# Two-bank score tiles and a new step plan in an attention and mixture-of-experts kernel

## The chip, the cores and the metric

The kernel runs on one core of a Trainium2 chip. The metric is the device time of one execution in microseconds (us). PE is TensorE (its weight loads are shown as PEld), DVE is VectorE, ACT is ScalarE, POOL is GpSimd, SP is the engine that issues most DMAs. PSUM, where PE writes, has 8 banks of 512 float32 in each of 128 partitions.

## What is computed

32 sequences of 256 tokens, model width 128. Each is layer-normed, then goes through one decoder block and a mixture of experts:

```python
x = layer_norm(hidden, ln1)                       # hidden: the layer norm of the input
hidden = attn(split_heads(q, k, v of x), causal) @ attn_proj_w + attn_proj_b + hidden
x = layer_norm(hidden, lnx)
hidden = attn(q of x, k and v of the encoder, logits added, tril + 2) @ x_proj_w + x_proj_b + hidden
hidden = hidden + gelu(layer_norm(hidden, ln2) @ fc_w + fc_b) @ mlp_proj_w + mlp_proj_b
x = x_input + layer_norm(hidden)
out = x + layer_norm(shared expert + top 2 of 8 experts, each (silu(a) * b) @ w2, of layer_norm(x))
```

Attention has 16 heads of width 8. The encoder's 256 keys and values are the same for all sequences. The softmax subtracts each query's own maximum.

## The kernel before, in words

The program has three stages: attention (lines 200 to 676), the MLP with the gate (line 786 on), the experts (line 909 on). Only the first one is changed.

Heads are laid out in four row groups of 32 partitions (g) with four heads each (j). A score product takes 32 partitions of one group and 128 columns of the array, so four products, one of each group, can run side by side. Each float32 query or key is kept as three bfloat16 parts, and the spare rows of a head hold the causal mask. Scores are computed twice. `maxima` (line 420) writes them by query into `sc` tiles, adds the mask on the diagonal with `strips`, and VectorE takes each query's negated maximum (line 443). `split` (446) makes three bfloat16 parts of the maxima on POOL, and `turned_maxima` (457) transposes them on PE. `weights` (477) computes the scores by key into `st` tiles, adds the maxima with `pick`, and ScalarE takes the exponential into `wt` (503). `weighted` (513) sums the values, 128 partitions by 32 columns of the array, into one `av` tile; a column of ones gives the softmax's sum. `back` (536) transposes and divides (547, 548), `turned_back` (551) transposes again, `joined` (559) multiplies by the output weights and adds to `h_all`.

Before all that a sequence is loaded (350), normed (`normed_in`, 361: statistics on VectorE, the power -0.5 on POOL in `rsqrt`, line 186), transposed (`turned`, 382), and projected (`projections`, 387). `projected` (240) splits queries and keys into parts on POOL (250 to 253), stores them in DRAM and loads them again in the layout of the heads, all by DMAs of the SP queue. `values` (404) makes the value tile `vpad`. For a self sequence `normed_in` makes two normed copies with two powers: `xn`, and the row `h_all` (lines 372 to 376); `biased` (378) adds the output bias to `h_all` on POOL.

A sequence's query work is cut into halves (412), one step each: 6 for a self, 8 for a cross sequence; its key work likewise (465). A half has two groups, so two `sc` tiles or two `st` tiles of one bank each. All PSUM tiles of all stages come from one pool of 8 banks, `ps` (159).

The order on PE is written out by hand: the loop at 662 takes two steps together, issues the products of up to two query halves and two key halves interleaved by group (`issue`, 569), then the reductions and exponentials (`after`), then the extra pieces of the two steps, with `weighted` last. VectorE, ScalarE and POOL are ordered by the framework, which also decides which free bank or buffer a tile gets, and each engine works strictly in its order. The steps come from the planner at 587 to 661: `on` puts a piece at a step, `full` at an even step, moved by one pair if a pair's cost passes 1.9. A sequence's key halves start LAG = 13 steps after its query halves; at most AHEAD = 7 sequences are begun and not yet at their cross attention; query and key buffers are used again after 4 sequences. In the regular part of the plan 14 steps (7 pairs) hold one self and one cross sequence.

## Time and profile before

| what | us |
|---|---|
| median of three runs | 1599.27 (1598.25 to 1602.11) |
| the profiled execution | 1591.84 |
| its span, first to last instruction | 1590.1 |
| PE busy | 1407.4 (89%) |
| PEld busy | 1099.7 (69%) |
| DVE busy | 1054.3 (66%) |
| ACT busy | 870.9 (55%) |
| POOL busy | 653.1 (41%) |
| DVE maxima, line 443, 896 instructions | 496.2 |
| ACT exponentials, line 503, 896 instructions | 420.7 |

The profiled execution is one run with the hardware profiler on. "Busy" is the time in which an engine executed something; matmuls are pipelined, so a busy PE is not PE at its peak. A row of the timeline has the start in us from the start of the span, the time in us, engine, source line, operation, output<-input, shape, the count of equal instructions that were merged, and in brackets the idle time before with what ended it. A row of the waits says which engine waited for what: us in total, times, longest. "issue" is time in which an engine waited for nothing that the profile shows.

### The profile page before, as it was taken

What the parts mean: (1) busy time and instruction counts of PE and PEld (TensorE: products, weight loads), DVE (VectorE), ACT (ScalarE), POOL (GpSimd) and SP (SyncE); (2) the same over time, 40 slices, a digit from 0 to 9 for tenths busy, and PEclk for the clock granted to TensorE, in tenths of its full rate; (3) what the DMA queues carried; (4) which work ended last, traced back from release to release, by engine and by line L of the source; (5) the groups of instructions that cost most, each with busy time, mean ns of one, the idle gap of its engine ahead of it and who ended that gap; (6) DMA issues with size and microseconds to landing.
All of it is one profiled execution on the core that took longest, in us unless ns stands there. A gap on an engine that the chain in (4) does not pass through costs nothing.

```text
span 1590.1 us, 74601 instructions
## 1 busy us (share of the span) xinstructions
PE 1407.4 (89%) x32988; PEld 1099.7 (69%) x32988; DVE 1054.3 (66%) x2955; ACT 870.9 (55%) x2032; POOL 653.1 (41%) x1475
## 2 busy tenths in 40 slices
PE   3678898898988988888999899799979999999997
PEld 2566677776777777777777787478756666666664
DVE  5647667776677776677776666267866666666665
ACT  1353566665666666666666655677734443433433
POOL 7435445444445444444444322378631212222112
PEclk8788999999999999999999989899979999999998
DMA  5632223232232232232222200500000000000000
GB/s 140 189 99 79 65 91 101 65 115 77 71 115 73 91 100 66 84 103 64 93 89 82 66 16 28 148 20 1 1 1 8 7 14 14 8 14 14 7 14 14
DMA packets 106037, 97.27 MB, mean 61 GB/s; under 512 B 4764, under 2 KB 105360, under 8 KB 105712
## 3 DMA queue, kind: packets, MB, share of 16 engines
q1 hardware_dynamic: 104432, 91.49, 18.7%
q8 instruction: 258, 4.23, 1.1%
q10 hardware_dynamic: 1280, 1.01, 0.2%
q14 instruction: 67, 0.55, 0.1%
HBM read 54.47 MB, written 37.77 MB: 58 GB/s over the span
## 4 chain that ended last, share of the span: by engine, by line
PE 66%; DVE 18%; POOL 6%; ACT 4%; issue 3%; DMA 3%; SPq 0%; POOLq 0%; ACTq 0%; DVEq 0%
DVE m L443 11%; PE av L525 11%; PE sc L580 9%; PE po L940 8%; PE pa L929 8%; PE pb L930 8%; PE st L580 7%; PE po L844 4%; PE pf L837 3%; PE pq L245 2%; POOL r L191 2%; ACT wt L503 2%; DVE st L182 2%; PE pa L541 1%; DVE xn L195 1%
## 5 line engine op out<-in xcount | busy, mean ns | idle before, releaser
L443 DVE TENSOR_REDUCE m<-sc 128x2 f32<-128x512 f32 (+2 forms) x896 | 496.2, 607 | 236.8 <-PE sc L580 207.3
L503 ACT ACTIVATE wt<-st 128x512 f32<-128x512 f32 (+1 forms) x896 | 420.7, 539 | 261.1 <-PE st L580 199.8
L580 PEld LDWEIGHTS <-qs 32*128 32x128 bf16 x6144 | 226.4, 95 | 96.7 <-issue 83.5
L580 PE MATMUL st<-mT,pick 32*128 32x256 bf16 (+2 forms) x2048 | 242.7, 245 | 3.8 <-issue 3.7
L580 PEld LDWEIGHTS <-strips 32*128 32x128 bf16 x7424 | 190.2, 94 | 21.8 <-issue 18.4
L940 PEld LDWEIGHTS po<-w,h 128*128 128x128 f32 x1152 | 154.7, 191 | 67.9 <-issue 49.5
L580 PE MATMUL sc<-kr,qs 32*128 32x256 bf16 (+1 forms) x3072 | 165.6, 250 | 33.4 <-DMA kr<-k 24.7
L580 PE MATMUL st<-qs,kr 32*128 32x128 bf16 (+1 forms) x3072 | 179.3, 248 | 8.3 <-issue 4.8
L580 PE MATMUL st<-qs,krx 32*128 32x130 bf16 (+1 forms) x3072 | 177.6, 243 | 7.4 <-issue 5.6
L580 PE MATMUL sc<-krx,qs 32*128 32x256 bf16 (+1 forms) x3072 | 178.9, 246 | 5.6 <-issue 2.6
L934 DVE SCALAR_TENSOR_TENSOR h<-pb,cols,sa 128x512 f32<-128x512 f32 x144 | 107.9, 749 | 113.7 <-ACT sa L932 88.8
L932 ACT ACTIVATE sa<-pa,cols 128x512 f32<-128x512 f32 x144 | 99.7, 693 | 147.3 <-PE pa L929 120.4
L940 PE MATMUL po<-w,h 128*128 128x128 f32 x1152 | 161.9, 277 | 0.0
L929 PE MATMUL pa<-h_all,w 128*128 128x512 f32 x288 | 150.7, 605 | 0.0
L930 PE MATMUL pb<-h_all,w 128*128 128x512 f32 x288 | 147.9, 595 | 0.0
L580 PE MATMUL sc<-strips 32*128 32x64 bf16 (+2 forms) x3840 | 140.2, 193 | 6.5 <-issue 6.4
L580 PE MATMUL st<-strips 32*128 32x64 bf16 (+2 forms) x3584 | 137.2, 193 | 8.7 <-issue 8.6
L954 POOL TENSOR_TENSOR z<-z 128x512 f32<-128x512 f32 x32 | 40.7, 1271 | 245.9 <-ACT z L950 245.9
L525 PE MATMUL av<-wt,vpadx 128*32 128x128 f32 (+1 forms) x4096 | 111.5, 252 | 32.2 <-DVE m L443 28.6
L191 POOL TENSOR_TENSOR r<-r,nhalf 128x2 f32<-128x2 f32 (+1 forms) x160 | 133.0, 837 | 9.9
L580 PEld LDWEIGHTS <-kr 32*128 32x128 bf16 x3072 | 118.1, 95 | 16.7 <-issue 13.9
L525 PEld LDWEIGHTS av<-wt,vpadx 128*32 128x32 f32 x4096 | 97.8, 112 | 44.4 <-DVE m L443 36.6
(162 smaller groups left out, 2649.8 us busy)
## 6 DMA issues: line engine op xcount, KB each, us to landing
kr<-k SPq DMA_DIRECT2D x32, 768.0 KB
k<-qkp SPq DMA_DIRECT2D x32, 576.0 KB
qs<-q SPq DMA_DIRECT2D x64, 256.0 KB
q<-qkp SPq DMA_DIRECT2D x64, 192.0 KB
x<-in_x_dram SPq DMA_DIRECT2D x32, 128.0 KB
x_all<-in_x_dram SPq DMA_DIRECT2D x8, 512.0 KB
out_dram<-y SPq DMA_DIRECT2D x16, 256.0 KB
w<-in_rw_dram SPq DMA_DIRECT2D x1, 1024.0 KB
```

What stands on the lines that cost most here:

```text
L191: nc.gpsimd.tensor_tensor(r, r, nhalf[:, 0:n], ALU.pow)
L443: nc.vector.tensor_reduce(m[:, g, js[0] : js[0] + n], t3, AX.X, ALU.max, negate=True)
L503: nc.scalar.activation(w[:, 0 : n * nq], t, AF.Exp)
L525: nc.tensor.matmul(av[32 * g : 32 * g + 32, j // 2, to : to + n], lhsT=self.vp[:, kb, g, WINDOW[j] : WINDOW[j] + 32], rhs=self.wts[kb, g, ...
L580: nc.tensor.matmul(dst, lhsT=lhsT, rhs=rhs, start=start, stop=False, skip_group_check=True)
L837: nc.tensor.matmul(pf, lhsT=wfc[:, f * P : (f + 1) * P], rhs=self.xT, start=True, stop=True)
L844: nc.tensor.matmul(po[:, i, :], lhsT=self.g[:, f, i * P : (i + 1) * P], rhs=wmlp[:, f, :], start=f == 0, stop=f == FF // P - 1)
L929: nc.tensor.matmul(pa, lhsT=w1[:, e, 0:D], rhs=rhs, start=True, stop=True)
L930: nc.tensor.matmul(pb, lhsT=w1[:, e, D : 2 * D], rhs=rhs, start=True, stop=True)
L932: nc.scalar.activation(sa, pa, AF.Silu, bias=col(C_B1 + 2 * e))
L934: nc.vector.scalar_tensor_tensor(h, pb, col(C_B1 + 2 * e + 1), sa, ALU.add, ALU.mult)
L940: nc.tensor.matmul(po[:, i, :], lhsT=h[:, i * P : (i + 1) * P], rhs=w2[:, e, :], start=True, stop=e < NE)
```

## The change

Six things are changed, all in attention:

- An `sc` tile is one tile of two banks for both groups of a half, and one VectorE reduction covers both.
- PSUM is cut for this stage into two such `sc` tiles (4 banks) and a pool of 4 banks for everything else. The pool of 8 is opened for the later stages.
- For a self sequence VectorE prepares both powers side by side, POOL takes one power of 128x4 (exponents 0.5 and -0.5), and `h_all` is made from `xn` with the output bias in one VectorE instruction. `biased` is left for cross sequences alone.
- The planner: LAG 15, AHEAD 8, pieces start earlier (loads at 28 steps ahead for 22, norms at 24 for 18), `weighted` has pairs of its own, which `full` avoids, and the plan is made four times so that it knows them. `turned_maxima` stands at least a pair later. Query and key buffers are free at the end of the key halves, and projections wait for that.
- `wt` tiles have two sizes: 18 of 512 columns and 8 of 260, for 22 of 512.
- Some preparations are moved: the two bias products to the head of PE's order, the clearing of the maxima frames behind the first four sequences' norms.

```diff
+    phalf = const.tile([P, 2, 2], F32, name="halves")
+    nc.gpsimd.memset(phalf[:, 0, :], 0.5)
+    nc.gpsimd.memset(phalf[:, 1, :], -0.5)
...
-    ps = ctx.enter_context(tc.tile_pool(name="ps", bufs=8, space=PSUM))
...
+        rings["sc"] = actx.enter_context(tc.tile_pool(name="ps_sc", bufs=2, space=PSUM))
+        rings["ps"] = actx.enter_context(tc.tile_pool(name="ps_a", bufs=4, space=PSUM))
...
-                    r1 = rsqrt(wk, mv, 1.0, EPS, "a")
-                    r2 = rsqrt(wk, mv, 1.0 + EPS, EPS * EPS, "b")
+                    r = wk.tile([P, 2, 2], F32, tag="rab", name="r")
+                    ratio, r2 = r[:, 0, :], r[:, 1, :]
+                    nc.vector.tensor_scalar(r2, mv[:, :, 1], 1.0 + EPS, EPS * EPS, ALU.mult, ALU.add)
+                    nc.vector.tensor_scalar(ratio, mv[:, :, 1], 1.0, EPS, ALU.mult, ALU.add)
+                    nc.vector.reciprocal(ratio, ratio)
+                    nc.vector.tensor_tensor(ratio, ratio, r2, ALU.mult)
+                    nc.gpsimd.tensor_tensor(r, r, phalf, ALU.pow)
                     for t in range(2):
                         normed(self.xn[:, t, :], xs[t], mv, r2, t)
-                        normed(self.hs[t], xs[t], mv, r1, t)
+                        nc.vector.scalar_tensor_tensor(self.hs[t], self.xn[:, t, :], ratio[:, t : t + 1],
+                                                       out_bias[False][:, 0, :], ALU.mult, ALU.add)
...
+                t4 = rings["sc"].tile([P, 2, 512], F32, tag="sc", name="sc")[:, :, 0 : n * nk].rearrange(
+                    "p g (c k) -> p g c k", k=nk)
...
-                    for g, t3 in tiles:
-                        nc.vector.tensor_reduce(m[:, g, js[0] : js[0] + n], t3, AX.X, ALU.max, negate=True)
+                    nc.vector.tensor_reduce(m[:, 2 * gp : 2 * gp + 2, js[0] : js[0] + n], t4, AX.X, ALU.max, negate=True)
...
+                def price(e):
+                    return max(0, filled.get(e, 0) + cost - 2.3) + 0.5 * (e in taken) + 0.02 * (e - step)
+
+                e = min(range(step + step % 2, max(step + step % 2, step + reach) + 1, 2), key=price)
...
-            e = full(s - 14, 0.35, x.turned)
-            e = full(e + 2, 0.5 if x.cross else 0.9, x.projections)
+                e = max(s - lead + 4, free.get(qk, -99) - 2)
+                e = full(e, 0.5, x.turned, reach=s - 10 - e)
+                e = max(e + 2, free.get(qk, -99))
+                e = full(e, 0.6 if x.cross else 1.1, x.projections, reach=s - 8 - e)
...
-                e = full(last + 3, 0.13, x.turned_maxima, qb)
+                    e = full(last + 4, 0.13, x.turned_maxima, qb, reach=s + LAG - 3 - last - 4)
...
-            free[x.cross, "qk", x.b % QK_BUFS] = end + 14
+                free[qk] = end + 1
...
-            e = full(half + 1, 1.2 if x.cross else 0.9, x.weighted, 0)
-            e = full(max(e, end + 1), 1.8, x.weighted, 1)
+                e = columns(half + 1, x.weighted, 0)
+                e = columns(max(e + 2, end + 1), x.weighted, 1)
...
-            first[x.b] = e + 20
+                first[x.b] = e + (26 if x.b >= SOON else 16)
...
-        on(-13, max_frames, False)
-        on(-9, out_biases)
+            on(-3, max_frames, False)
+            on(-26, out_biases)
```

More of the change, by code (lines that the diff above doesn't have):

```diff
@@ L27 @@
 NEG = -1e30
-LAG = 13
+LAG = 15
 V_BUFS = 4
 QK_BUFS = 4
-AHEAD = 7
+AHEAD = 8
+SOON = 2
 COLS = ["ln1_g", "ln1_b", "lnx_g", "lnx_b", "ln2_g", "ln2_b", "bq", "bk", "bqx", "bkx", "bv", "bvx"]
@@ L156, in transformer_moe_kernel, with bank @@
     nc.vector.tensor_scalar(bqs[:, 1:2], c_of["bqx"], SCALE, None, ALU.mult)
-    ps = ctx.enter_context(tc.tile_pool(name="ps", bufs=8, space=PSUM))
-    def bank(name):
-        return ps.tile([P, 512], F32, tag="ps", name=name)
+    rings = {}
+    def bank(name, dtype=F32, n=512):
+        return rings["ps"].tile([P, n], dtype, tag="ps", name=name)
     out_bias = {cross: const.tile([P, 1, D], F32, name=f"out_bias{int(cross)}") for cross in (False, True)}
@@ L200, in transformer_moe_kernel @@
     with ExitStack() as actx:
+        rings["sc"] = actx.enter_context(tc.tile_pool(name="ps_sc", bufs=2, space=PSUM))
+        rings["ps"] = actx.enter_context(tc.tile_pool(name="ps_a", bufs=4, space=PSUM))
         wk = actx.enter_context(tc.tile_pool(name="wk", bufs=3))
         wl = actx.enter_context(tc.tile_pool(name="wl", bufs=5))
-        wtp = actx.enter_context(tc.tile_pool(name="wtp", bufs=22))
+        wtp = actx.enter_context(tc.tile_pool(name="wtp", bufs=1))
         kx = actx.enter_context(tc.tile_pool(name="kx", bufs=1))
@@ L371, in normed_in @@
                     mv = moments(wk, xs, "a")
-                    r1 = rsqrt(wk, mv, 1.0, EPS, "a")
-                    r2 = rsqrt(wk, mv, 1.0 + EPS, EPS * EPS, "b")
+                    r = wk.tile([P, 2, 2], F32, tag="rab", name="r")
[5 more added lines that the diff above has]
+                    nc.gpsimd.tensor_tensor(r, r, phalf, ALU.pow)
                     for t in range(2):
                         normed(self.xn[:, t, :], xs[t], mv, r2, t)
-                        normed(self.hs[t], xs[t], mv, r1, t)
+                        nc.vector.scalar_tensor_tensor(self.hs[t], self.xn[:, t, :], ratio[:, t : t + 1],
+                                                       out_bias[False][:, 0, :], ALU.mult, ALU.add)
             def biased(self):
                 h = h_all[:, 2 * self.b : 2 * self.b + 2, :]
-                nc.gpsimd.tensor_tensor(h, h, out_bias[self.cross].to_broadcast([P, 2, D]), ALU.add)
+                nc.gpsimd.tensor_tensor(h, h, out_bias[True].to_broadcast([P, 2, D]), ALU.add)
             def turned(self):
@@ L426, in maxima @@
                 m = self.ms[qb]
-                work, tiles = {}, []
+                work = {}
+                t4 = rings["sc"].tile([P, 2, 512], F32, tag="sc", name="sc")[:, :, 0 : n * nk].rearrange(
+                    "p g (c k) -> p g c k", k=nk)
                 for g in (2 * gp, 2 * gp + 1):
                     st = slice(32 * g, 32 * g + 32)
-                    t3 = bank("sc")[:, 0 : n * nk].rearrange("p (c k) -> p c k", k=nk)
-                    tiles.append((g, t3))
+                    t3 = t4[:, g % 2]
                     todo = [(nk, t3[:, c, :], self.qs[st, j, qb * P : qb * P + P], self.kr[st, j, part, 0:nk],
@@ L459, in turned_maxima @@
                     self.mT = wl.tile([P, S], BF16, tag="mT", name="mT")
-                pt = ps.tile([P, P], BF16, tag="ps", name="pt_m")
+                pt = bank("pt_m", BF16, P)
                 nc.tensor.transpose(pt, self.mp[qb].rearrange("p g r -> p (g r)"), ident_b)
@@ L501, in after @@
                     for g, t in tiles:
-                        w = wtp.tile([P, 512], F32, tag="wt", name="wt")
+                        cols, bufs = (512, 18) if n * nq > 260 else (260, 8)
+                        w = wtp.tile([P, cols], F32, tag=f"wt{cols}", name="wt", bufs=bufs)
                         nc.scalar.activation(w[:, 0 : n * nq], t, AF.Exp)
@@ L584, in transformer_moe_kernel @@
         pairs = [(Attention(b, False), Attention(b, True)) for b in range(NB)]
-        extra, filled = {}, {}
-        def on(step, f, *args):
-            extra.setdefault(step, []).append((f, args))
-        def full(step, cost, f, *args):
-            e = step + step % 2
-            if filled.get(e, 0) + cost > 1.9 and filled.get(e + 2, 0) < filled.get(e, 0):
-                e += 2
-            filled[e] = filled.get(e, 0) + cost
-            on(e, f, *args)
-            return e
-        by_query, by_key, first, free = {}, {}, {}, {}
@@ L602, in transformer_moe_kernel @@
-        at = begun = ended = 0
-        cross = True
-        while ended < NB:
-            ready = ended < begun and first[ended] <= at
-            cross = begun == NB or (ready and not cross) or begun - ended == AHEAD
-            if cross:
-                x = pairs[ended][1]
-                at = max(at, first[ended])
-                ended += 1
-            else:
-                x = pairs[begun][0]
-                begun += 1
-            at = max(at, *(free.get((x.cross, what, x.b % n), at) for what, n in (("qk", QK_BUFS), ("v", V_BUFS))))
-            at += at % 2
-            halves, keys = x.query_halves(), x.key_halves()
-            s = at
-            at += len(halves)
-            if not x.cross:
-                on(s - 22, x.load)
-            on(s - 18, x.normed_in)
-            if x.b < QK_BUFS:
-                on(s - 17, x.spares)
-            on(s + 2, x.biased)
-            e = full(s - 14, 0.35, x.turned)
-            e = full(e + 2, 0.5 if x.cross else 0.9, x.projections)
-            assert e <= s - 8, (e, s)
-            if not x.cross:
-                full(e + 2, 0.55, x.values)
-            for i, h in enumerate(halves):
-                by_query[s + i] = (x, h)
-            for qb in range(2):
-                last = s + max(i for i, h in enumerate(halves) if h[0] == qb)
-                on(last + 1, x.split, qb)
-                e = full(last + 3, 0.13, x.turned_maxima, qb)
-                assert e < s + LAG
-            for i, h in enumerate(keys):
-                by_key[s + LAG + i] = (x, h)
-            end = s + LAG + len(keys)
-            free[x.cross, "qk", x.b % QK_BUFS] = end + 14
-            half = end if x.cross else s + LAG + sum(h[0] == 0 for h in keys)
-            e = full(half + 1, 1.2 if x.cross else 0.9, x.weighted, 0)
-            e = full(max(e, end + 1), 1.8, x.weighted, 1)
-            free[x.cross, "v", x.b % V_BUFS] = e + 12
-            e = full(e + 2, 0.5, x.back)
-            e = full(e + 2, 0.25, x.turned_back)
-            e = full(e + 2, 0.6, x.joined)
-            first[x.b] = e + 20
@@ L651, in transformer_moe_kernel, with planned, on, full @@
-        on(-18, spares)
-        on(-15, diagonals)
-        on(-13, max_frames, False)
-        on(-11, picks)
-        on(-9, out_biases)
-        full(-5, 0.5, encoder_turned)
-        on(-5, logit_parts)
-        on(-4, encoder_rows)
-        full(-2, 0.5, encoder_keys)
-        full(0, 0.5, encoder_values)
-        on(2, max_frames, True)
+        def planned(taken):
+            extra, filled, by_query, by_key, first, joined, free = {}, {}, {}, {}, {}, {}, {}
+            def on(step, f, *args):
+                extra.setdefault(step, []).append((f, args))
+            def full(step, cost, f, *args, reach=10):
+                def price(e):
+                    return max(0, filled.get(e, 0) + cost - 2.3) + 0.5 * (e in taken) + 0.02 * (e - step)
+                e = min(range(step + step % 2, max(step + step % 2, step + reach) + 1, 2), key=price)
+                filled[e] = filled.get(e, 0) + cost
+                on(e, f, *args)
+                return e
+            def columns(step, f, *args):
+                e = step + step % 2
+                own.add(e)
+                on(e, f, *args)
+                return e
+            own = set()
+            at = begun = ended = 0
+            cross = True
+            while ended < NB:
+                ready = ended < begun and first[ended] <= at
+                cross = begun == NB or (ready and not cross) or begun - ended == AHEAD
+                if cross:
+                    x = pairs[ended][1]
+                    at = max(at, first[ended])
+                    ended += 1
+                else:
+                    x = pairs[begun][0]
+                    begun += 1
+                qk, v = (x.cross, "qk", x.b % QK_BUFS), (x.cross, "v", x.b % V_BUFS)
+                at = max(at, free.get(qk, -99) + 10)
+                at += at % 2
+                halves, keys = x.query_halves(), x.key_halves()
+                s = at
+                at += len(halves)
+                if not x.cross:
+                    on(s - 28, x.load)
+                lead = min(24, s - joined[x.b] - 2) if x.cross else 24
+                on(s - lead, x.normed_in)
+                if x.b < QK_BUFS:
+                    on(s - 23, x.spares)
+                if x.cross:
+                    on(s + 2, x.biased)
+                e = max(s - lead + 4, free.get(qk, -99) - 2)
+                e = full(e, 0.5, x.turned, reach=s - 10 - e)
+                e = max(e + 2, free.get(qk, -99))
+                e = full(e, 0.6 if x.cross else 1.1, x.projections, reach=s - 8 - e)
+                assert e <= s - 8, (e, s)
+                if not x.cross:
+                    full(max(e + 2, free.get(v, -99)), 0.55, x.values)
+                for i, h in enumerate(halves):
+                    by_query[s + i] = (x, h)
+                for qb in range(2):
+                    last = s + max(i for i, h in enumerate(halves) if h[0] == qb)
+                    on(last + 1, x.split, qb)
+                    e = full(last + 4, 0.13, x.turned_maxima, qb, reach=s + LAG - 3 - last - 4)
+                    assert e < s + LAG
+                for i, h in enumerate(keys):
+                    by_key[s + LAG + i] = (x, h)
+                end = s + LAG + len(keys)
+                free[qk] = end + 1
+                half = end if x.cross else s + LAG + sum(h[0] == 0 for h in keys)
+                e = columns(half + 1, x.weighted, 0)
+                e = columns(max(e + 2, end + 1), x.weighted, 1)
+                free[v] = e + 2
+                e = full(e + 2, 0.5, x.back)
+                e = full(e + 2, 0.25, x.turned_back)
+                e = full(e + 2, 0.6, x.joined)
+                joined[x.b] = e
+                first[x.b] = e + (26 if x.b >= SOON else 16)
+            on(-24, spares)
+            on(-21, diagonals)
+            on(-3, max_frames, False)
+            on(-17, picks)
+            on(-26, out_biases)
+            full(-5, 0.5, encoder_turned, reach=2)
+            on(-5, logit_parts)
+            on(-4, encoder_rows)
+            full(-2, 0.4, encoder_keys, reach=2)
+            full(0, 0.4, encoder_values)
+            on(8, max_frames, True)
+            return extra, by_query, by_key, own
@@ L662, in transformer_moe_kernel @@
+        own = set()
+        for _ in range(4):
+            extra, by_query, by_key, own = planned(own)
         with tc.manual_schedule(engines={mybir.EngineType.PE}):
@@ L676, in transformer_moe_kernel @@
                 s += 2
+    rings["ps"] = ctx.enter_context(tc.tile_pool(name="ps", bufs=8, space=PSUM))
     late = ctx.enter_context(tc.tile_pool(name="late", bufs=1))
@@ L917, in spread @@
         def spread(self):
-            pw = ps.tile([P, P], BF16, tag="ps", name="pw")
+            pw = bank("pw", BF16, P)
             nc.tensor.transpose(pw, cwp[:, self.c * CH : (self.c + 1) * CH, :].rearrange("p t r -> p (t r)"), ident_b)
```

## The prediction

> **What bounds the kernel now.** I read the stretches by windows first, then the waits of the regular part, then the timeline of one sequence on each engine, then the chain of waits of the start.

> ```profile
> 0.00:199.30 199.30, 134.10 (x3793) 111.28 (x3793) 123.09 (x314) 80.39 (x191) 102.89 (x251) 0.85 0.39 114
> 199.30:895.50 696.20, 618.97 (x22607) 529.35 (x22606) 491.15 (x1222) 444.54 (x1079) 325.35 (x845) 1.00 0.28 87
> 895.50:1012.60 117.10, 105.96 (x3762) 89.46 (x3761) 67.00 (x176) 69.88 (x177) 28.50 (x94) 0.95 0.08 24
> 1012.60:1590.10 577.50, 548.39 (x2832) 369.63 (x2832) 373.04 (x1246) 276.05 (x587) 196.40 (x286) 0.96 0.07 20
> ```

> Columns: stretch, its length, busy PE, PEld, DVE, ACT, POOL, clock, DMA. Attention ends at 1012.6; the last 577.5 us (MLP, experts) are not touched by the change beyond names. Of the 1012.6, 696.2 is regular: 24 equal turns of the plan, 29.0 us each, a turn being 14 steps (7 step pairs) with one self and one cross sequence. PE is the busiest, but DVE (71%) and ACT (64%) are not far.

> In the timeline of PE every turn is the same row of pieces, so each piece has a least and a median length over 24 turns. Medians: seven score blocks (L580) 1.86, 1.57, 1.84, 1.58, 3.38, 3.79, 2.25; four value sums (L525) 1.01, 1.88, 1.28, 1.89; whole-array products 6.1 together; in all 28.4, the mean being 29.0. The least: blocks 1.86, 1.57, 1.71, 1.45, 2.06, 1.99, 2.00 (for the fifth, which never ran free, I put the least of another block of 100 products), 12.6; sums 6.1; whole-array 5.5; in all 24.2. So 4.8 us a turn is waiting, 3.1 of it in the fifth and sixth blocks. Why those two:

> ```profile
> 592.54 0.41 DVE L565 TENSOR_TENSOR h_all<-po,h_all 128x256 f32<-128x256 f32 x1
> ...
> 593.91 2.46 DVE L443 TENSOR_REDUCE m<-sc 128x2 f32<-128x512 f32 x4
> ...
> 599.05 0.60 DVE L195 TENSOR_SCALAR h_all<-x,mv,r 128x128 f32<-128x128 f32 x2 [1.89 <-POOL r L191]
> 599.57 2.48 DVE L443 TENSOR_REDUCE m<-sc 128x4 f32<-128x512 f32 x4
> ```
> ```profile
> 600.31 1.96 PE L525 MATMUL av<-wt,vpadx 128*32 128x128 f32 x64 [1.30 <-DVE m L443]
> ```
> ```profile
> 598.31 1.38 POOL L191 TENSOR_TENSOR r<-r,nhalf 128x2 f32<-128x2 f32 x2
> ```

> DVE holds four reductions a pair (2.48), then the join and statistics (1.37) ahead of the next four, then stands 1.89 for a power on POOL with four reductions queued behind it. All PSUM is one pool of 8 banks, one pair fills it (4 score, 4 st tiles), so the value sum at 600.31 waits for a bank that DVE has not read. The waits of the regular part (us in total, times, longest) agree:

> ```profile
> PEld av L525 <- DVE m L443: 38.7, 65, 1.9
> DVE h_all L195 <- POOL r L191: 37.8, 20, 1.9
> ```

> The start is bound by POOL and by DMAs queued behind it:

> ```profile
> 50.74 0.56 POOL qkp L250
> ...
> 54.45 8.23 DMA q<-qkp
> ```

> The third sequence's keys come so late that the block at 50.95 lasts 13.5 us, where its 152 products need about 3.

> **The change, part by part.** I make the sum on the profiled execution's own 1591.84 us; the median of three runs, 1599.27, is 7.4 above it, and the difference is carried over.

> *Reductions over two banks.* 28 reductions a turn become 14. Four of 128x512 take 2.48, so one follows another after 0.60, and two of 128x260 take 0.76, one after 0.34: 1.03 ns an element and about 0.067 fixed. Per turn 14 x 0.067 = 0.9 us of DVE is saved. [...] Against it, a double tile frees its banks after 1.13 + 0.08, not 0.68. No row shows one instruction over two banks: bounds 1.13 and 1.36 (no saving at all); I take 1.13, being the same stream of elements.

> *Two score tiles, four other banks.* [...] A pair now fills all four other banks with st tiles, so every value sum and whole-array product waits for an exponential of the same pair. Row of ACT: four exponentials 2.06 in all, one each 0.49, the first ending 0.60 after its start. The first two st tiles are complete about 1.1 to 1.4 us into a 2.0 us block (the exponential of the block at 602.20 starts at 603.59), so the first bank is free at 1.7 to 2.05 and the fourth at 3.2 to 3.5. [...]

> *The order.* The plan, worked out for 32 sequences, gives this turn: four pairs with a block and one value sum (one of them with a pt_m transpose), then pairs with (a) two backs, two pt_m, values, pt_x; (b) two pt_a, pq, pt_x; (c) two joins, pt_m, pq for q and k. I laid out the engines' queues in the built order with the rows' lengths. The four sum pairs run free: DVE has 2.3 us of reductions against 3.0 to 3.9 us of PE. (a): pv and pt_x take the banks of the two pt_m, whose ACT copies (0.27 each) follow the fourth exponential: 0.4 waited. (b): its second st tile takes pt_x's bank: 0.57 of ACT after pt_x, 0.75 waited. (c) itself is free, but the next block's second st tile takes the first join's bank, and DVE is last there: from (a) on it holds reductions 1.7 + 2.3 + 2.3, backs 1.7, norms and statistics about 3, joins 0.8, against some 11.5 on PE: 0.7 waited. Smaller ones 0.25. Sum 2.1. Whole-array products next to value sums: pt_a before a sum takes 0.51, elsewhere 0.17, and pt_x 0.60 for 0.37; the plan has two such neighbours fewer, which the 24.2 counts already, and a new one of 0.2 (pt_m). So 24.2 + 0.2 + 2.1 = 26.5. Irregular waits ("issue" inside blocks, median over least and mean over median) were about 1.0 a turn; I keep 0.9. 27.4 against 29.0: 1.6 a turn, 24 turns, 38 us.

> *A sequence's rows on VectorE.* Off POOL: two multiply-adds 0.19, two powers 0.70, a bias add 0.72, for one power of 128x4 at 1.04 (row of L191, 128x4): 1.5 a sequence less. Onto DVE: four ops of 128x2, not shown, bounds 0.05 and 0.25 each (the 128x16 reciprocal is 0.25); 0.1 taken. The new product for h, 128x128, lies between 0.26 and 0.34 (y L957), as the 0.30 it replaces. The 1.89 stand goes because the built order of DVE puts the power's users most of a turn after it. Late next is DVE's own stretch (a) to (c), counted above.

> *Transposed maxima a pair later, LAG 15.* Takes 8 us of waiting for mparts out at most; nothing where the start hides it. Cross query loads get four pairs (15 us) instead of six: pq at 617.9, q stored from 621.6, load issued 623.5, about 9 us to landing, so free; SP's order puts no other transfer between.

> *Start.* POOL's powers and multiply-adds before the first split are 7.5 us, then four powers of about 1.04: 3 less. The third sequence's projection now stands ahead of the first scores, so its 10 us goes; the fourth's keys, about 52 us, are next late. Of the later blocks over 6 us (four, 28.5 us, 20 of it waiting for keys) the lead is four or five pairs as before, so half goes: 10. Sum 23, bounds 5 and 40. *End* (117 us): 2.

> Sum 38 + 23 + 2 = 63: 1529 for the profiled execution, 1536 for the median.

> **Rivals.** (1) *The stand moves.* DVE cannot keep up from (a) to (c), as double tiles free late and ACT and DVE stands add: a turn of 28.4, 0.6 x 24 = 14, and a start that gains 12. 1599 - 26 = 1573. For it: DVE's load there is above PE's. Against: it has 4 us idle in the sum pairs. (2) *Slower: four banks are too few.* If the first exponential ends late, each pair stands 0.73 (0.60 and a hand-over): 7 x 0.73 = 5.1, a turn of 24.4 + 2.1 + 5.1 + 0.6 = 32.2, 3.2 x 24 = 77 lost, 25 of it won back at the start: 1651. It decides from 0.25 us late per pair on, where the 1.6 is gone. For it: ACT is at 64% and takes 16 copies a turn between exponentials. Against: first tiles are complete mid-block. (3) *No net change*: the start wins nothing and the turn 0.

> **Numbers.** Forecast 0.60; (1) 0.22; (2) 0.13; (3) 0.05. About 0.3% (5 us) is what a measurement can tell from no change. Faster 0.82, same 0.05, slower 0.13. The range: low end with the waits at 1.3 a turn and 40 at the start, 1599 - 58 - 40 = 1501; high end past (1), 1590, where what is left out is (2), (3) and a little of (1).

> **What would show it.** Right: a turn near 27.4; no h_all wait on POOL; reductions near 1.2 each; the sum pairs' pieces at their least; the first value sum near 60 us, not 73.6; the MLP stage at 577 us. Wrong: value sums waiting for ACT wt in every pair (2); blocks after (c) waiting for DVE joins by over 1 us (1); a two-bank reduction of 1.36 or more, or long blocks for the fourth to eighth sequence's keys.

## The result and the profile after

The changed kernel takes 1673.81 us (median of 4, 1658.46 to 1678.88) where the kernel before took 1598.76 (4 runs on the same chip): 1.0467 times as long, 95% interval 1.0381 to 1.0552. It is slower by some 75 us; forecast were 1536.

The profiled execution of after took 1678.88 us, its span is 1677.2. The windows of after, in the columns of the windows of before; attention now ends at 1099.9:

```profile
0.00:233.30 233.30, 166.25 (x4706) 135.67 (x4706) 149.90 (x356) 99.68 (x235) 106.33 (x246) 0.88 0.41 122
233.30:973.80 740.50, 615.33 (x21641) 518.64 (x21638) 467.55 (x913) 425.49 (x1030) 274.49 (x731) 0.98 0.24 75
973.80:1099.90 126.10, 106.32 (x3821) 88.37 (x3814) 63.41 (x121) 70.27 (x180) 24.94 (x87) 1.00 0.06 19
1099.90:1677.20 577.30, 548.18 (x2832) 369.86 (x2832) 373.07 (x1246) 275.94 (x587) 195.97 (x285) 0.96 0.07 20
```

The last stage is as it was. For the rest, before has to be cut so that about the same products stand in each part: at the first value sum of its eighth self sequence (228.7 us) and 23 turns later. After is cut at that of its ninth, since its plan begins one more sequence ahead; PE's counts in the three parts then agree within 2%:

```profile
0.00:228.70 228.70, 160.01 (x4735) 133.31 (x4738) 143.74 (x367) 99.15 (x236) 116.87 (x287) 0.87 0.37 111
228.70:895.50 666.80, 593.06 (x21665) 507.31 (x21664) 470.50 (x1169) 425.78 (x1033) 311.37 (x809) 0.99 0.28 87
```

The head is 4.6 us longer (233.3 for 228.7), the 23 regular turns 73.7 longer (740.5 for 666.8), the end 9.0 longer (126.1 for 117.1). Together 87.3, which is where the end of attention went, from 1012.6 to 1099.9. So most of the loss is in the regular turn: 32.2 us, not 29.0 and not 27.4. PE's clock, 0.98 for 0.99, can be only a small part of 11%.

PE's largest waits in the regular part of after (us in total, times, longest):

```profile
PEld L596 <- issue: 144.7, 304, 2.2
PE st L596 <- issue: 31.7, 33, 2.0
PEld av L541 <- issue: 25.9, 25, 3.5
PE st L596 <- DVE h_all L581: 22.0, 22, 1.2
PE sc L596 <- issue: 20.8, 25, 2.1
PE av L541 <- issue: 20.4, 22, 3.4
PEld av L541 <- ACT wt L519: 15.2, 42, 0.6
PEld pv L293 <- ACT mT L476: 11.1, 21, 0.5
```

The two rows that the prediction built on, the sums waiting for maxima and `h_all` for POOL, are gone. The rows that have grown most name no engine: "issue" on PE's score blocks (L596) and sums (L541). The rows of that kind in before (199.3 to 895.5 us, 24 turns):

```profile
PEld L580 <- issue: 86.5, 243, 2.7
PE st L580 <- issue: 21.9, 33, 2.5
PE sc L580 <- issue: 11.3, 21, 1.2
PEld av L525 <- issue: 4.6, 12, 1.0
PE av L525 <- issue: 1.9, 4, 0.9
```

VectorE's part did what it should. After the power on POOL nothing stands, as its timeline shows. A reduction over two banks of 512 columns takes 1.23 us alone, and two in a row take 2.35:

```profile
634.26 0.34 DVE L389 SCALAR_TENSOR_TENSOR h_all<-xn,r,out_bias 128x128 f32<-128x128 f32 x1
634.52 0.34 DVE L200 TENSOR_SCALAR xn<-x,mv,r 128x128 f32<-128x128 f32 x1
634.89 0.35 DVE L389 SCALAR_TENSOR_TENSOR h_all<-xn,r,out_bias 128x128 f32<-128x128 f32 x1
```
```profile
631.23 1.23 DVE L457 TENSOR_REDUCE m<-sc 128x4 f32<-128x1024 f32 x1 [0.56 <-POOL mr L469]
...
640.29 2.35 DVE L457 TENSOR_REDUCE m<-sc 128x4 f32<-128x1024 f32 x2
```

PE's timeline of an ordinary moment of after has holes in the middle of a block, before products for which the profile names nothing that they waited for:

```profile
621.18 0.23 PE L596 MATMUL st<-strips 32*128 32x128 bf16 x2 [0.96 <-issue]
...
625.48 0.28 PE L596 MATMUL st<-mT,pick 32*128 32x256 bf16 x2 [1.09 <-issue]
```

PE's own instructions come by DMA. The page of after lists that queue beside the others (packets, MB, share):

```profile
q8 instruction: 258, 4.23, 1.0%
```

4.23 MB in 258 packets are 16,384 bytes each. PE runs 32,988 products and as many weight loads, 65,976 instructions, which is 257.7 times 256: a packet holds 256 of them, 64 bytes each. The trace has each packet's time. Around the two holes (my reading of the packets and of PE's rows):

```
fetch 618.72, took 0.92      hole 620.22 to 621.18
fetch 623.08, took 1.01      hole 624.39 to 625.48, 256 PE instructions after the one before
fetch 627.12, took 0.93
```

The holes end 1.54 and 1.39 us after a fetch has ended, and 256 instructions lie between them. In the traces of this study two fetches never start less than 3.23 us apart (3.27 in before, 3.31 in after; in the regular turns the middle one of the distances is 3.80 in before and 4.20 in after). So in every one of them at least 3.23 us passed per 256 instructions, 128 products.

The two holes stand for many. With PE's products and loads numbered in their order, all 70 idle times of PE over 0.3 us that end with "issue" in the 23 regular turns of after lie at one place of a block of 256, within two instructions (the place moves by one a turn), and each ends 0.86 to 1.60 us after a fetch has ended, the middle one 1.40. They are 70.6 us together. In the 23 turns of before there are 45, with 31.8 us. So 39 of the 73.7 us are such holes.

To see where a turn loses, I took each piece of it (a block, a sum, whole-array products) over all turns of the most common form. The sum of the least lengths ("leasts") is the turn as it would be without irregular waits; it moves by up to 0.5 us with where exactly a piece is said to end.

| kernel | products | mean turn | sum of leasts | above the least |
|---|---|---|---|---|
| before | 942 | 29.0 | 24.8 | 4.2 |
| after | 942 | 32.6 | 26.0 | 6.6 |

(The 32.2 includes four turns of other forms.) The leasts grew by 1.2 us, and what stands above them by 2.4. Within one row the pieces of after are a clockwork wherever whole-array products stand: 0.88, 0.75, 0.44, 0.42, a block of 2.27, 0.56, 0.32, 0.52, a block of 1.88. They vary only from the joins on: the block behind them 2.53 to 3.8, the blocks of the sum pairs 2.0 to 4.6, the sums themselves 1.0 to 5.1.

### The profile page after: what moved, and what is told of

It is laid out like the page before. It is cut to its first block, busy times and chain, and to the rows that moved or that the text cites. A ratio compares the mean times of both kernels' runs of the same rounds, so it can differ in the third digit from the quotient of the medians.

```text
span 1677.2 us, 73976 instructions
## 1 busy us (share of the span) xinstructions
PE 1436.1 (86%) x32988; PEld 1112.5 (66%) x32988; DVE 1053.9 (63%) x2635; ACT 871.4 (52%) x2032; POOL 601.7 (36%) x1349
## 3 DMA queue, kind: packets, MB, share of 16 engines
q8 instruction: 258, 4.23, 1.0%
q10 hardware_dynamic: 1280, 1.01, 0.2%
## 4 chain that ended last, share of the span: by engine, by line
PE 65%; DVE 17%; issue 8%; ACT 5%; DMA 2%; POOL 2%; SPq 0%; POOLq 0%; ACTq 0%; DVEq 0%
PE av L541 12%; PE st L596 11%; DVE m L457 8%; PE sc L596 8%; PE po L979 8%; PE pa L968 8%; PE pb L969 7%; ACT wt L519 4%; PE po L883 3%; PE pf L876 3%; DVE xn L200 2%; DVE st L187 1%; DVE mv L188 1%; PE pv L293 1%; PE pq L252 1%
## 5 line engine op out<-in xcount | busy, mean ns | idle before, releaser
L457 DVE TENSOR_REDUCE m<-sc 128x4 f32<-128x1024 f32 (+2 forms) x448 | 468.6, 1070 | 355.6 <-PE sc L596 297.1
L596 PEld LDWEIGHTS <-qs 32*128 32x128 bf16 x6144 | 230.9, 96 | 140.6 <-issue 133.1
L596 PE MATMUL st<-mT,pick 32*128 32x256 bf16 (+2 forms) x2048 | 246.4, 245 | 11.6 <-issue 11.6
L596 PEld LDWEIGHTS <-strips 32*128 32x128 bf16 x7424 | 193.3, 95 | 31.5 <-issue 29.2
L596 PE MATMUL sc<-kr,qs 32*128 32x128 bf16 (+1 forms) x3072 | 170.9, 255 | 44.2 <-DVE m L457 31.1
L596 PE MATMUL st<-qs,kr 32*128 32x128 bf16 (+1 forms) x3072 | 180.7, 244 | 32.0 <-DVE h_all L581 23.2
L596 PE MATMUL st<-qs,krx 32*128 32x130 bf16 (+1 forms) x3072 | 184.4, 248 | 22.3 <-issue 8.0
L596 PE MATMUL sc<-krx,qs 32*128 32x256 bf16 (+1 forms) x3072 | 179.3, 246 | 9.1 <-issue 7.5
L467 POOL CAST mparts<-m 128x16 bf16<-128x16 f32 x128 | 25.2, 196 | 422.6 <-DVE m L457 422.0
L596 PE MATMUL sc<-strips 32*128 32x64 bf16 (+2 forms) x3840 | 141.8, 194 | 13.2 <-issue 12.9
L596 PE MATMUL st<-strips 32*128 32x64 bf16 (+2 forms) x3584 | 140.8, 194 | 11.4 <-issue 11.4
L596 PEld LDWEIGHTS <-krx 32*128 32x128 bf16 x3072 | 116.0, 93 | 36.0 <-issue 30.8
L596 PEld LDWEIGHTS <-kr 32*128 32x128 bf16 x3072 | 119.1, 93 | 12.8 <-issue 12.2
L541 PE MATMUL av<-wt,vpad 128*32 128x128 f32 x3072 | 108.9, 285 | 20.4 <-issue 15.0
```

What stands on the lines that cost most here:

```text
L457: nc.vector.tensor_reduce(m[:, 2 * gp : 2 * gp + 2, js[0] : js[0] + n], t4, AX.X, ALU.max, negate=True)
L541: nc.tensor.matmul(av[32 * g : 32 * g + 32, j // 2, to : to + n], lhsT=self.vp[:, kb, g, WINDOW[j] : WINDOW[j] + 32], rhs=self.wts[kb, g, ...
L596: nc.tensor.matmul(dst, lhsT=lhsT, rhs=rhs, start=start, stop=False, skip_group_check=True)
```

## The experiments

Theories: the *instruction stream* (PE is short of instructions where many small products stand in a row); the *cut of PSUM* (four banks for everything but scores are too few); the *double tile* (two banks free late); and *VectorE* (the stand moves). All ratios are to before on the same chip.

**The rows alone.** Before, with the new rows on VectorE, and the bias products at the head of the order:

```diff
-                    r1 = rsqrt(wk, mv, 1.0, EPS, "a")
-                    r2 = rsqrt(wk, mv, 1.0 + EPS, EPS * EPS, "b")
...
+                    nc.gpsimd.tensor_tensor(r, r, phalf, ALU.pow)
...
-        on(-9, out_biases)
+        on(-20, out_biases)
```

> The kernel before with the rows' part alone: one power of 128x4 on POOL, the rest of the self norm on VectorE (the bias products are moved ahead of it). If the 1.89 us stand of VectorE behind the power in each turn is worth what the waits say, 20 to 45 us less than before: 1555 to 1580. If other waits take its place: 1590 to 1600.

1582.41, ratio 0.9917 (0.9892 to 0.9943): the only faster version of the full computation. Yet in the profiled execution the regular part is no shorter: 228.7 us of head became 221.2, and the 23 turns 669.4 for 666.8:

```profile
221.20:890.60 669.40, 597.95 (x21665) 507.20 (x21664) 488.07 (x1249) 428.38 (x1033) 282.72 (x733) 1.00 0.28 86
```

The stand is gone (no `h_all` wait on POOL is left), the sum of leasts is 24.3, the medians of the pieces add up to 27.55 against 28.36, and the mean turn is 29.1 against 29.0: what the medians won, irregular waits took back.

**The old plan with the new tiles** (LAG 13, AHEAD 7 and the planner of before in after), and the same with single tiles:

```diff
-LAG = 15
+LAG = 13
...
-        rings["sc"] = actx.enter_context(tc.tile_pool(name="ps_sc", bufs=2, space=PSUM))
+        rings["sc"] = actx.enter_context(tc.tile_pool(name="ps_sc", bufs=4, space=PSUM))
...
-                    nc.vector.tensor_reduce(m[:, 2 * gp : 2 * gp + 2, js[0] : js[0] + n], t4, AX.X, ALU.max, negate=True)
+                    for g, t3 in tiles:
+                        nc.vector.tensor_reduce(m[:, g, js[0] : js[0] + n], t3, AX.X, ALU.max, negate=True)
```

(The second and third hunks are of the second run alone.)

> The changed kernel with the old planner (LAG 13, AHEAD 7, sums beside whole-array pieces); two-bank score tiles, four other banks and the rows on VectorE stay. Theory S (supply): PE's instructions arrive in fetches of 256, at least 3.3 us apart, and four pairs in a row of nothing but small products outrun them; then the old plan brings the time back to 1550 to 1600. Theory B (banks): value sums and whole-array products wait in the pool of four banks; then it stays at 1650 or goes above. Theory D (double tiles free late on VectorE): 1630 or more.

> The plan of before, the rows on VectorE, and PSUM cut 4 + 4 as in after, but the four score banks are single tiles with a reduction each. Against the rows alone (1582) the cut with double tiles cost 39 us (1621). If the loss is the cut itself (value sums, whole-array products and key scores share four banks and wait for the exponentials), this stays at 1612 to 1630. If it is the double tile (its two banks come free only when the one long reduction ends), it falls to 1580 to 1592. I expect the first, since the waits of that run name the exponentials three times as often as the maxima.

1621.03 (1.0164; 1.0125 to 1.0204) with double tiles, 1629.35 (1.0192; 1.0150 to 1.0234) with single ones. Against single tiles the double tile costs nothing that these runs can tell. The cut, 4 banks for scores and 4 for the rest, costs 39 to 44 us over the rows alone (by the ratios). The first run's 1621 lies above what the stream theory had set (1550 to 1600) and below the other two (1630 and 1650 or more). In the profiled executions of that run and of the rows alone half of the difference is in the 23 turns (18.6 of the 36 us of attention), the rest in the head and the end. Both runs also have the two sizes of `wt`; that is no rival, since exponentials wait for sums to free a `wt` buffer 0.3 us in all there, and 22.4 us in the rows alone. Waits of the first of the two (240 to 860 us):

```profile
PEld pq L251 <- ACT wt L518: 15.4, 19, 0.9
...
PEld av L540 <- ACT wt L518: 10.7, 38, 0.3
...
PEld pv L292 <- ACT wt L518: 9.7, 20, 0.5
PEld po L578 <- ACT wt L518: 7.9, 18, 0.5
```

Projections, values, joins and sums all wait for an exponential to give up a bank, each a little, about once a turn (the sums twice): leasts 25.0 for 24.3, mean turn 29.9.

**The plan of after in one pool of 8, the sums not apart, and both.** The first has one pool, single tiles and two reductions, the second loses the line that marks a sum's pair as taken:

```diff
-        rings["sc"] = actx.enter_context(tc.tile_pool(name="ps_sc", bufs=2, space=PSUM))
-        rings["ps"] = actx.enter_context(tc.tile_pool(name="ps_a", bufs=4, space=PSUM))
+        rings["ps"] = actx.enter_context(tc.tile_pool(name="ps_a", bufs=8, space=PSUM))
...
                 e = step + step % 2
-                own.add(e)
                 on(e, f, *args)
```

> The changed kernel with one pool of 8 banks, one-bank score tiles and two reductions a half, as before; the new plan and the rows on VectorE stay. Theory S: nothing of the plan is undone, so 1645 to 1690, as the changed kernel. Theories B and D: the loss goes, 1540 to 1590.

> The changed kernel, but the planner no longer knows which pairs hold value sums, so whole-array pieces go beside them again; LAG 15 and the leads stay. Theory S: most of the loss goes, 1560 to 1620. Theories B and D: no gain, 1650 to 1690.

> The plan of after with the sums not kept apart, one pool of 8 banks, single tiles with a reduction each, the rows on VectorE. If the two losses add (cut of PSUM about 39, sums apart about 50), it lands at 1580 to 1595, beside the rows alone (1582). If earlier pieces and LAG 15 are worth something once both are gone, it is below 1575. If the plan costs something in other ways than by keeping the sums apart, above 1600.

One pool: 1639.36 (1.0289; 1.0260 to 1.0319). Not apart: 1626.10 (1.0205; 1.0176 to 1.0233). Both: 1620.27 (1.0128; 1.0085 to 1.0172).

The first and the second miss their forecasts by 6 us, and both lie on the side of the stream theory. Not keeping the sums apart is worth some 2.6% of the time (1.6% in one pool), and where it comes from is plain: the leasts of a turn are 25.8, nearly as in after (26.0), and the mean is 29.9 for 32.6. Nearly all of it is irregular waiting. One pool is worth 1.8% under the plan of after and 0.8% with the sums not apart.

The losses do not simply add (that would have given 1580 to 1595); the third run came out in the branch above 1600, where the plan costs something in another way. In one pool it has a wait of its own. These are the waits of the third run (240 to 860), and its timeline at such a place:

```profile
PEld pq L251 <- DVE m L456: 46.6, 21, 2.5
```
```profile
642.62 2.47 DVE L456 TENSOR_REDUCE m<-sc 128x4 f32<-128x512 f32 x4
643.35 0.30 PEld L251 LDWEIGHTS pq<-xT,wqx 128*128 128x128 f32 x2 [2.47 <-DVE m L456]
```

Every turn, a projection needs a bank that holds scores, and VectorE, busy with joins, norms and the four small operations of the rows, comes to them 2.2 us late. That is the rival "the stand moves", 2.2 x 24 = 53 us by the row, in a version where it is not hidden. In after the projection has no such wait, since scores have their own banks, and the block behind the joins waits instead.

**Fewer products at the same columns.** The causal mask is added by products for strips 32 scores wide, 232 of the 942 products of a turn. Two of them are made one, 64 wide; the triangle then can't be kept, so each is compared with a base run that has the narrow strips and leaves the triangle out too. The edit on the side of the keys (that of the queries is alike; `quarter`, 0.25 everywhere, stands for the triangle in the base runs already):

```diff
-                    for a in range(4):
+                    for a in range(0, 4, 2):
...
-                        w = 32 - skip
+                        w = 64 - skip
-                        todo.append((n * w, t3[:, :, at + skip : at + 32], eye[st, a, :],
-                                     tri_k[st, skip:32].unsqueeze(1).to_broadcast([32, n, w]), False))
+                        todo.append((n * w, t3[:, :, at + skip : at + 64], eye[st, a, :],
+                                     quarter[st, skip:64].unsqueeze(1).to_broadcast([32, n, w]), False))
```

> After, with the triangle of the causal mask left out: the same mask products run, but add 0.25 everywhere. Only a base for the next run; every theory expects the time of after, within 8 us.

> As the run before, but two mask products of 32 columns are one of 64: the same columns, and 112 products, 224 of some 1880 PE instructions, fewer in a turn, 12%. Theory of the instruction stream: the turns of after lose most of what they lose to waits for instructions, 30 to 60 us below the run before. If only the engine's own time or the waits for banks count: within 12 us of it.

> Before, with the triangle of the causal mask left out in the same way. A base; the time of before within 8 us.

> Before with two mask products of 32 columns as one of 64 and the triangle left out. Theory of the instruction stream: a gain here too, 15 to 40 us below its base, but smaller than in after by 15 us or more, because the value sums of before stand beside whole-array products, which need few instructions for their time. Otherwise: the same gain in both, under 12 us.

| kernel | us | ratio (interval) | products | mean turn | leasts |
|---|---|---|---|---|---|
| after, base | 1664.96 | 1.0490 (1.0449 to 1.0531) | 942 | 32.1 | 26.0 |
| after, wide | 1613.58 | 1.0143 (1.0087 to 1.0199) | 830 | 29.5 | 25.9 |
| before, base | 1589.82 | 1.0008 (0.9987 to 1.0029) | 942 | 28.7 | 24.8 |
| before, wide | 1561.90 | 0.9838 (0.9812 to 0.9865) | 830 | 28.0 | 25.1 |

In after 51 us go, in before 28, as the stream theory had forecast (30 to 60; 15 to 40), and the leasts hardly change (25.9 for 26.0 in after, 25.1 for 24.8 in before): in a free turn no cost of the products that are left out can be told. Only the waiting above the leasts shrinks, from 6.1 to 3.6 us in after. This is what the instruction stream says and what a theory of banks or of VectorE does not. In before, wide, mean (27.96) and sum of medians (27.96) are the same: hardly anything irregular is left, and what stands above the least is its two blocks that wait for VectorE.

**The stream by itself.**

```python
for cols, n in ((64, 2560), (128, 2560), (256, 1536)):
    for i in range(n):
        nc.tensor.matmul(t4[i % 4][:, 0:cols], lhsT=w[st, :], rhs=x[st, 0:cols], ...)   # st: row group i % 4
```

> Does none of the reference's work (the output is zeros). PE alone: 2560 score-like products (32 partitions by 128 columns of the array, row groups in turn) of 64 columns, 2560 of 128 and 1536 of 256, no waits inside a stretch, each stretch after a long pause. Theory of the instruction stream: PE's instructions come in blocks of 256 that never start closer than 3.3 us, so after a first burst from what was fetched in the pause the stretches of 64 and of 128 columns settle at the same 128 products in 3.3 us, 26 ns each, and the one of 256 columns runs at PE's own pitch. Rival (PE's own pitch binds): the pitch is the same from the first product on and grows with the columns.

PE's timeline in the stretch of 64 columns, then of 128 (whose first row comes after the pause), then of 256:

```profile
28.78 1.90 PE L67 MATMUL t<-x,w 32*128 32x64 bf16 x128 [1.83 <-issue]
32.23 1.89 PE L67 MATMUL t<-x,w 32*128 32x64 bf16 x128 [1.56 <-issue]
35.69 1.89 PE L67 MATMUL t<-x,w 32*128 32x64 bf16 x128 [1.56 <-issue]
```
```profile
101.06 7.44 PE L67 MATMUL t<-x,w 32*128 32x128 bf16 x351 [14.46 <-DVE x L73]
109.73 1.97 PE L67 MATMUL t<-x,w 32*128 32x128 bf16 x128 [1.23 <-issue]
113.46 1.97 PE L67 MATMUL t<-x,w 32*128 32x128 bf16 x128 [1.76 <-issue]
```
```profile
187.71 39.49 PE L67 MATMUL t<-x,w 32*128 32x256 bf16 x1375 [14.49 <-DVE x L73]
```

With no wait in the program PE runs 128 products, stands for mostly 1.5 to 2.0 us, and runs the next 128. A block of 128 takes 3.45 to 4.0 us, 27 to 31 ns a product, though PE needs 15 ns for one of 64 or of 128 columns; at 256 columns (28.7 ns) the gaps are nearly gone. After the pause 351 products ran without one, 702 instructions. The granted clock is not the reason, as the page's row of tenths shows (40 slices of 6.2 us):

```profile
PEclk9985555555555555599997999999555999999955
```

In the stretch of 64 columns (18 to 86 us) it was 0.5, in that of 128 (101 to 173 us) 0.9 but for the first slice (0.5) and one of 0.7, and the blocks of 128 products take 3.45 us or more in both.

**The rows once more, with fewer products,** and a version that keeps the mask, in strips of 64 rows by 64 columns (the edit shown is that of the second, key side):

```diff
-                    for a in range(4):
+                    for a in range(2):
...
-                        w = 32 - skip
-                        todo.append((n * w, t3[:, :, at + skip : at + 32], eye[st, a, :],
-                                     tri_k[st, skip:32].unsqueeze(1).to_broadcast([32, n, w]), False))
+                        w = 64 - skip
+                        two = slice(64 * (g % 2), 64 * (g % 2) + 64)
+                        todo.append((n * w, t3[:, :, at + skip : at + 64], eye[two, a, :],
+                                     tri_k[two, skip:64].unsqueeze(1).to_broadcast([64, n, w]), False))
```

> The rows on VectorE alone, with two mask products of 32 columns as one of 64 (triangle left out, 0.25 added), so 112 products of 942 fewer in a turn. Before in that form took 1562, its turn 27.9. With the full count of products the rows took DVE's 1.89 stand out of every turn and the turn stayed at 29.1. If the instruction stream took that gain back, it must show here: a turn of 27.0 or less, 1562 - 12 for the head and tail - 20 for 24 turns: 1525 to 1540. If the stand was simply replaced by another wait for VectorE: a turn of 27.7 to 28, 1548 to 1555.

> A full version: the rows on VectorE alone, and the causal mask in strips of 64 rows and 64 columns, so that two mask products become one and the triangle is kept. A product now holds 64 partitions, so of the four groups only two can run masks side by side. If the number of products decides, it lands within 10 us of the run before it, at 1525 to 1550, and is the fastest of all. If the array's time decides (a mask takes two groups' rows), at 1560 to 1590.

The first: 1540.40 (0.9616; 0.9584 to 0.9649), a turn of 27.4 against the 28.0 of before in that form. So with fewer instructions the removed stand does shorten the turn, by some 0.5 us, where with all of them it did nothing. The turn lies between the two expectations, 27.0 and 27.7: the stream had taken back part of the gain, not all. The largest wait for VectorE that is left on PE is that of the transposes of normed rows (`pt_x`) for a bank of scores, 10.0 us in 23 turns.

The second is slower: 1740.67 (1.0874; 1.0835 to 1.0912), far above both of its forecasts. It counts 830 products too, but the leasts of its score blocks are 0.7 to 1.7 us longer. The groups show the weight loads of the mask strips, first of this version (64 rows), then of the one before (32 rows), with the idle time ahead of them behind the second bar:

```profile
L590 PEld LDWEIGHTS <-strips 64*128 64x128 bf16 x3840 | 140.5, 94 | 158.7 <-issue 71.8
```
```profile
L591 PEld LDWEIGHTS <-strips 32*128 32x128 bf16 x3840 | 150.4, 95 | 6.3 <-issue 3.2
```

The loads of 64 rows take as long as those of 32 (94 ns for 95), but PEld stands 158.7 us ahead of them against 6.3; why stays open. The run is useful for another reason: its turn is 33.9 on the mean, and 33.9 as a sum of leasts. With PE slowed, the irregular waits are gone. I read them as those of a PE that is faster than its instructions.

**Where PE stands, in all of them.** PE's idle times over 0.1 us in 23 regular turns, by what the profile says ended them. Those over 0.3 us that end with "issue" lie at the ends of blocks of 256 in each of these runs, as in after:

| kernel | 23 turns, us | idle, "issue" | idle, an engine or DMA named | PE busy |
|---|---|---|---|---|
| before | 666.8 | 34.7 | 35.3 | 593.1 |
| rows alone | 669.4 | 43.9 | 23.5 | 598.0 |
| rows alone, PSUM cut (old plan, double tiles) | 688.0 | 39.4 | 33.9 | 610.1 |
| after | 740.5 | 73.4 | 46.9 | 615.3 |
| after, sums not apart | 684.0 | 29.5 | 35.5 | 611.1 |
| after, one pool | 709.9 | 66.0 | 40.4 | 602.9 |
| after, both | 690.6 | 22.1 | 56.3 | 609.2 |
| before, wide | 643.1 | 4.9 | 50.0 | 584.9 |
| after, wide | 674.2 | 24.2 | 52.4 | 594.3 |

In the rows alone the waits for an engine fell by 11.8 us and the holes grew by 9.2: that is where most of the gain went. The cut of PSUM alone brings no more holes, but 10.4 us of waits for an engine, and PE's rows cover 12.1 us more. Keeping the sums apart costs 43.9 us of holes with the cut and as much in one pool; where it is undone in one pool, waits for an engine take 15.9 of it back.

## Why the prediction was wrong, step by step

*What bounds the kernel.* The waits in the fifth and sixth block were read rightly, and counted wrongly as pure loss. 942 products and 942 loads are 7.4 fetches, at 3.23 us, the shortest distance seen, some 24 us a turn, by chance the prediction's sum of least pieces (24.2). While PE stands its instructions go on coming in: in the stream run 702 of them ran without a hole after 14.46 us of standing. The rows alone fit that: VectorE's stand for POOL gone, turn unchanged (29.1 for 29.0), more holes (43.9 us for 34.7).

*"The four sum pairs run free."* This is the step that failed. VectorE and ScalarE did leave them nearly free, but kept apart from whole-array products they make, from the block behind the joins to the next whole-array products, a stretch of 716 products with one other between. 1,432 instructions are 5.6 fetches, at 3.23 us each some 18 us; PE's leasts there are 16.7; measured were some 22.5 on the mean, 3.1 of it holes: 69.2 of the 70.6 us of holes lie in the 22 such stretches. The prediction put the supply of instructions at nothing, without a reason. In before the longest such stretch had 448, with two others between, and VectorE's two stands lay in it.

*"I keep 0.9."* The term for irregular waits was the mis-sized one. They were carried over as a constant, but grow with what else is taken away. The working's regular part, 26.5, holds: the sum of leasts is 26.0, within what the way of counting moves it. What stands above it is 6.6, of which about 1 is the block behind the joins (median 3.66 over a least of 2.53; I had 0.7 for that wait, it was 1.0 on the mean, and the sign named for it, over 1 us, is there with 1.2). Of the rest, holes for instructions are 3.1 a turn (1.4 in before). The runs agree: fewer products win 2.5 a turn, the sums not kept apart 2.7; these overlap.

*"Two score tiles, four other banks."* My estimate from ACT's row was that a value sum stands 0 to 0.1. It was a little more: sums and their loads wait for exponentials 8.1 + 15.2 us in 23 turns, on the mean at most 0.25 a sum. But the cut reaches all pieces, and with the old plan costs 39 to 44 us. The rival of four banks too few came nearest: its forecast of 32.2 us a turn is the time measured, but by luck, since its mechanism (0.73 us in every pair) is not there.

*Reductions over two banks:* 1.23 us alone, and 1.12 more for the second in a row, where I had 1.13: right, and worth nothing that the two runs with the old plan can tell. *Transposed maxima, LAG, AHEAD:* not tested alone.

*"Start".* Forecast were 23 us less; the head is 4.6 longer (and the end 9.0 longer for 2 less, which was not looked into). The wait for the third sequence's keys did go, as the waits up to the first turns show (after, 0 to 135 us, then before, 0 to 125):

```profile
PE sc L596 <- DVE m L457: 20.9, 16, 6.0
...
PE sc L596 <- DMA kr<-k: 7.6, 1, 7.6
```
```profile
PE sc L580 <- DMA kr<-k: 24.2, 3, 11.3
```

But with score blocks alone on PE, two double tiles are all that can be ahead of VectorE, where before eight single ones could, and the blocks stand 20.9 us for reductions, a row that before does not have there. The first value sum came at 83.7 us, not 60, and not 73.6.

*The supply of instructions.* The 27.4 has no term for it. In the stream run 128 products of 128 columns with their loads, 256 instructions, ran in 1.97 us, but in the rows shown a new block of 256 began only every 3.45 us or more. At 3.23 us a block, the shortest distance in the traces, a turn's instructions alone take some 24 of the 27.4, and a stretch that is much denser than the mean runs short, as that of the sum pairs did (22.5 us for leasts of 16.7).

What stays open: the 22 us by which PE's own rows cover more of the 23 turns than before (615.3 for 593.1, while a product's mean length is 239 ns for 237, so they overlap less), of which the cut alone brings some 12 and the rest is not placed; why a fetch does not start sooner; and whether the projection's wait is all of the 34 us (2.1%) that the plan with sums not apart costs in one pool over the rows alone.

## What to carry to other kernels

Count instructions as well as columns: divide the number of PE's products and loads in a stage by 256, take 3.23 us or more for each block, the shortest distance in the traces here, and compare with PE's time there. Where the two are near, a wait taken away elsewhere can come back as "issue" (in the rows alone PE's waits for an engine fell from 35.3 to 23.5 us, and "issue" grew from 34.7 to 43.9). Then keep large products among the small ones (29.5 us of holes in the 23 turns of after with the sums not apart, 73.4 with them apart), and cut the number of products before the waits (12% fewer were worth 51 us in after and 28 in before). Before a wait is booked as a gain, ask what else was catching up while it lasted.
